# The end of layer 1: other scalar steps, the first twelve row sums of x times M on VectorE, and the squares of M summed by ScalarE

## The chip, the cores and the metric

The kernel runs on one core of one Trainium2 chip. The metric is the device time of one execution, in microseconds (us). The kernel before takes 496.52 us, the median of three runs (496.17 to 497.64).

A core has five engines that work at the same time and wait for each other by semaphores: TensorE (PE in the profile; PEld are its weight loads) multiplies matrices into a memory of eight banks called PSUM, VectorE (DVE), ScalarE (ACT) and GpSimd (POOL) do elementwise work, and SyncE (SP) issues most transfers from main memory.

## The reference

There are 3327 nodes with 64 features (x) and one dense weighted adjacency matrix `adj` (3327 x 3327). Four graph layers follow each other, each as `x = layernorm(x + gnn(x))`. Cut to what matters here:

```python
# layer 0:  x - 0.1 x + const per row
# layer 1, hyperbolic:
x_tan     = logmap0(x)
left      = x_tan @ att_W[:64] + att_b
right     = x_tan @ att_W[64:]
adj_att   = sigmoid(left + right.T) * adj
x_local   = logmap(x[:, None], x[None, :])           # every pair of nodes
support_t = einsum('ij,ijd->id', adj_att, x_local)
out       = proj(expmap(support_t, x))               # contains tanh(|support|)
# layer 2:  twice  x = tanh(concat([adj @ x, x], 1) @ W[k])
# layer 3:  decayed weights of the last 100 neighbours of each row, times (x @ weight), plus bias
```

For every pair of nodes in layer 1 `logmap` gives the direction from i to j in the ball: a number that depends on the pair times x_j, and another one times x_i. After the sum over j each row is therefore a combination of two vectors: of M, the weighted sum of the neighbours' vectors, and of x of the row itself. All that follows the sum (expmap, proj, the residual and the layer norm) needs per row only a few scalars: q, the sum of squares of M's row; p, the sum of x times M over the row; and t, M's last coordinate, which carries the sum of the weights. From these come two factors, alpha and beta, and the layer's output is alpha M + beta x, both centred.

## The kernel before

**Tiling.** The 3327 nodes are padded to 3328, which is 26 blocks of 128. The blocks are kept in pairs, b and b + 13, one in the upper and one in the lower half of the 128 partitions where a tile is transposed: such a tile has 64 + 64 partitions and 13 groups of 128 columns. A "slot" is the place of one block, a "group" is a pair of slots. Scalars per node are tiles of 128 x 26. The transposed tiles are worked on in four chunks of 416 columns (`CW`).

**Order.** Within layer 1 the orders of TensorE, ScalarE, VectorE and GpSimd are written out by hand (`tc.manual_schedule`): an engine runs its instructions in the order of the program text and waits at each for what it needs. Transfers have their own queue on SyncE. A pool of PSUM banks may take over the place of an earlier pool. It then waits for the last users of that place; for pools with `reuse_waits="tile"` this is kept by tile.

**The pairs, `near_sphere`.** Data that lie near a sphere, as these do, take this branch. Column halves `cp` (2), blocks of neighbours `jb` (26) and chunks within the half `ci` (2) make 104 tiles. For each tile:

- TensorE multiplies transposed left rows `riT` with the transposed neighbours `ljT` into `pq` (`products`, L1405). `ljT[1]` holds the same as `ljT[0]` with the partition halves changed.
- ScalarE takes an arctangent of it (`angle`, L1414) and, for each pair of tiles, the sigmoid `sg` of the attention (L1378). GpSimd multiplies `sg` by the adjacency `at` (L1383).
- VectorE makes the weights `v` (`gather`). For even tiles this is one instruction (L1429), for odd ones three (L1425, L1426, L1427).
- TensorE adds v times the block's rows `lj` to `acc` (`collect`, L1449), one PSUM bank for each chunk of the half. When the last block of a half is done, `acc` is copied to `mT`, chunk by chunk (L1455). `mT` is M, transposed. The last two of these copies come after the last tile, the first two in the middle of the layer, where the column half changes.

**The start of the branch.** The transposed operands are made at once, by transpositions into PSUM (`bank`, `alone`, `made`) followed by a copy to `riT`, `ljT[0]`, `ljT[1]` or `lfT`. `right` makes `ljT[0]`, `wrong` makes `ljT[1]` (its first tile is first_wrong in the profile), `turn` makes `riT`, `left_rows` makes `lfT`, which goes through main memory to spread `left` over the partitions. Where `right` copies a part of `ljT[0]`, two transfers on SyncE's queue (`change_over`) make the same part of `ljT[1]`. `seventh` is the last such part of the start: its tile, prep_right, stands in the first `acc` bank, and `by_rows` copies `lfT` from `prep_few`, which stands in the second `acc` bank. Both copies are in VectorE's order behind v of tile 0.

**The tail of the tiles.** Beside the last four tiles GpSimd makes `xm`, which is `mT` times `riT`, for the first half of the columns (L1632) and some scalars per row (`gs`, `gk`, `gsp`, `gs2`, `aav`). TensorE turns the first six groups of `mT` back to rows, by a product with the constant `all_m` (L1645), into `pq_early`: each group gives 128 columns of M and two of t. ScalarE squares these 768 values (`sq_e`, L1650) and copies t (`t_e`, L1654), ahead of the last two copies of `mT`. VectorE makes three scalars per row (`inv_s`, `rxn`, `xn`, L1657 to L1659), the second half of `xm` (L1661), and the row sums of `sq_e` (L1662), which are the first twelve columns of q.

**The end, `near_end`.** It has new pools on the PSUM banks of `acc` and `pq`. In TensorE's order stand: `pm` for groups 6 to 12 (L1720); `pe`, which is p of all 13 groups, each a product of 128 columns of `xm` with a constant of two columns, so 13 products, each shown as two records (L1740); `first_w` (a transposition of `all_m` and the product of the centring matrix with W, L1791 and L1792); `pm` for groups 0 to 2; `second_w` (W times the turned `all_m`, giving `w_m`, and the centred layer 3 weights `w3`, L1802 and L1803); `x_w`, centred x times W of most groups; `pm` for groups 3 to 5; more `x_w` and `m_w`, M times W (`times`, L1760). ScalarE squares `pm` into `sq_m` (L1734), copies M out (`m_out`, L1730) and `x_w` to `lj` (`x_out`, L1766). VectorE sums `sq_m` (L1778, L1779) and runs a chain of short steps of 128 x 26, of which this is the head:

```python
vec(k, p, gs, mul)            # L1786, e_k: the first that needs pe
vec(gp, p, gsp, mul)
vec(k, k, gt, add)
```

From this follow `u2` (the square of the length of support), `ux`, the argument of tanh, tanh on ScalarE (L1824) with two loads of function tables, of which the second is made early by a dummy instruction, e_warm; then `root` and its Sqrt on ScalarE (e_on_s, L1857), a second Sqrt (L1858 has both reciprocals), `alpha` and `beta`. Last comes, per part, `lj = alpha (M W) + beta (x W)` (L1895 to L1897). It is first done for group 0 alone.

**What comes behind.** Layer 2 needs this `lj`: its products with the adjacency (`cnt`, L517) begin with slot 0. The adjacency itself arrives by transfers that run ahead, four blocks of 1664 KB at a time.

## Time and profile before

| | |
|---|---|
| median of the runs | 496.52 us |
| the profiled execution | 496.15 us |
| its span, first to last instruction | 494.3 us |
| granted clock of TensorE, mean | 0.984 |
| TensorE busy | 478.6 us (97%) |
| VectorE busy | 349.8 us (71%) |
| ScalarE busy | 266.1 us (54%) |
| GpSimd busy | 196.8 us (40%) |
| pairs of layer 1 | about 21 to 189 us |
| end of layer 1, `pm` to `cnt` | 189.28 to 203.64 us |
| layers 2 and 3 | 203.64 to 494.3 us |

The span is measured from the first to the last instruction of one execution under the profiler; that execution itself took 496.15 us, so 1.85 us lie around the span. In all the rows that are shown, times are in microseconds, and "L1449" is line 1449 of the kernel before. In a timeline a row has the start, the length, the engine, the line, the operation, the output and input names with shape and type, and the number of instructions in it; in square brackets is the idle time just before and what ended it. A matrix product in float32 appears as two records. In the rows of the chain of waits only what set the end is listed: each row is followed back from the last instruction to what released it, or to what stood before it on its engine.

### The profile page before, as it was taken

How to read it: one execution, taken by the hardware profiler on the slowest of the kernel's cores; microseconds unless marked ns; L12 is line 12 of the kernel's file. 1: busy time of each engine (PE TensorE's matmuls, PEld its weight loads, DVE VectorE, ACT ScalarE, POOL GpSimd, SP SyncE). 2: the span in 40 equal slices, each digit the busy share in tenths (PEclk: the TensorE clock that was granted, in tenths of full speed). 3: DMA queues.
4: the chain of work that ended last, by engine and by line, in shares of the span. 5: the costliest groups of instructions: out<-in, count | busy, mean ns of one | idle time of the engine just before them, and what ended most of it. 6: DMA issues, size and time to landing. Idle time of an engine off the chain costs nothing.

```text
span 494.3 us, 7739 instructions
## 1 busy us (share of the span) xinstructions
PE 478.6 (97%) x2865; PEld 219.2 (44%) x2865; DVE 349.8 (71%) x600; ACT 266.1 (54%) x376; POOL 196.8 (40%) x175
## 2 busy tenths in 40 slices
PE   7999999999999999999999999999999999999991
PEld 4733333334333338644333353333345455555551
DVE  6888888878888887995544322645239999789743
ACT  4899999999999985300000000000016876676641
POOL 4398999989999991000000000000342274000000
PEclk9899999999999998999999999999999999999996
DMA  9998988887888178999998009998997699949001
GB/s 289 358 299 289 321 271 268 267 274 256 280 277 276 71 290 312 427 420 430 420 411 333 0 19 393 428 354 324 422 361 225 227 343 373 384 159 355 16 1 42
DMA packets 34186, 139.20 MB, mean 282 GB/s; under 512 B 11231, under 2 KB 13025, under 8 KB 29019
## 3 DMA queue, kind: packets, MB, share of 16 engines
q1 hardware_dynamic: 30603, 137.41, 74.3%
q10 hardware_dynamic: 2288, 0.57, 0.6%
q0 software_dynamic: 1248, 0.64, 0.6%
q8 instruction: 24, 0.39, 0.3%
q14 instruction: 23, 0.19, 0.1%
HBM read 136.93 MB, written 1.04 MB: 279 GB/s over the span
## 4 chain that ended last, share of the span: by engine, by line
PE 90%; DVE 4%; DMA 1%; issue 1%; ACT 0%; POOL 0%; DVEq 0%
PE cnt L517 30%; PE pq L1405 17%; PE acc L1449 16%; PE cnt L654 6%; PE acc L886 6%; PE acc L903 3%; PE t L452 2%; DVE mask L368 1%; PE both L755 1%; PE cnt L508 1%; DMA mask<-t_rows 1%; PE x_w L1760 1%; DVE w L670 1%; PE pn_l L403 1%; PE pm L1720 1%; PE m_w L1760 1%
## 5 line engine op out<-in xcount | busy, mean ns | idle before, releaser
L1383 POOL TENSOR_TENSOR sg<-sg,at 128x832 f32<-128x832 f32 x88 | 131.5, 1518 | 7.4 <-ACT sg L1378 3.3
L517 PE MATMUL cnt<-at_l,lj 128*64 128x416 f32 x496 | 90.7, 515 | 0.0
L1378 ACT ACTIVATE sg<-lb,rb 128x1664 f32<-128x1664 f32 (+1 forms) x53 | 88.1, 1664 | 0.0
L1405 PE MATMUL pq<-riT,ljT 64*128 64x416 f32 x416 | 87.3, 536 | 0.2
L1449 PE MATMUL acc<-v,lj 128*64 128x416 f32 x416 | 85.1, 525 | 0.0
L1414 ACT ACTIVATE pq<-pq 128x832 f32<-128x832 f32 x104 | 83.9, 852 | 1.7 <-issue 1.6
L633 ACT ACTIVATE x<-cnt 128x416 f32<-128x416 f32 x8 | 4.1, 517 | 143.1 <-PE cnt L517 143.1
L672 ACT ACTIVATE w<-cnt 128x416 int16<-128x416 f32 x135 | 63.9, 519 | 27.3 <-PE cnt L654 25.8
L1429 DVE SCALAR_TENSOR_TENSOR v<-pq,sg 128x832 f32<-128x832 f32 x52 | 53.3, 1025 | 18.7 <-ACT pq L1414 18.4
L464 POOL DMA_DIRECT2D t_rows<-tb x4 | 4.1, 1088 | 150.0 <-DVE tb L462 150.0
L1405 PEld LDWEIGHTS pq<-riT,ljT 64*128 64x128 f32 x416 | 35.6, 186 | 49.5 <-ACT pq L1414 30.6
L517 PEld LDWEIGHTS cnt<-at_l,lj 128*64 128x64 f32 x496 | 34.4, 137 | 49.6 <-issue 49.1
L886 PE MATMUL acc<-w,s 128*128 128x416 bf16 x208 | 53.1, 339 | 0.0
L670 DVE TENSOR_SCALAR w<-cnt 128x416 int16<-128x416 f32 x73 | 42.1, 588 | 11.1 <-PE cnt L654 8.7
L1449 PEld LDWEIGHTS acc<-v,lj 128*64 128x64 f32 x416 | 26.1, 136 | 52.1 <-issue 48.2
L517 PE MATMUL cnt<-kept,lj 128*64 128x416 f32 x224 | 41.4, 515 | 0.0
L368 DVE TENSOR_SCALAR mask<-ah 128x1664 bf16<-128x1664 f32 x34 | 37.2, 1120 | 0.2 <-DMA ah<-in_adjT 0.2
L654 PE MATMUL cnt<-mask,tri 128*128 128x416 bf16 x136 | 35.4, 339 | 1.1 <-DMA mask<-t_rows 0.5
L445 DVE TENSOR_SCALAR tm<-at_l 128x1664 bf16<-128x1664 f32 x16 | 15.7, 1023 | 25.8 <-PE t L452 25.8
L1426 DVE SCALAR_TENSOR_TENSOR pq<-pq,sg 128x416 f32<-128x416 f32 x52 | 31.2, 599 | 1.8
L1425 DVE SCALAR_TENSOR_TENSOR v<-pq,sg 128x416 f32<-128x416 f32 x52 | 30.2, 580 | 0.0
L1047 POOL DMA_DIRECT2D out<-hid x2 | 1.0, 514 | 72.8 <-DVE hid L1052 72.8
(321 smaller groups left out, 522.0 us busy)
## 6 DMA issues: line engine op xcount, KB each, us to landing
at_l<-in_adjT SPq DMA_DIRECT2D x27, 1664.0 KB, 11.7
at<-in_adjT SPq DMA_DIRECT2D x44, 832.0 KB, 6.5
ah<-in_adjT SPq DMA_DIRECT2D x34, 832.0 KB, 6.8
kept<-in_adjT SPq DMA_DIRECT2D x7, 1664.0 KB, 11.0
bt_l<-in_adjT SPq DMA_DIRECT2D x6, 1664.0 KB, 8.7
lb<-lf_rows SPq DMA_DIRECT2D x2, 384.0 KB
mask<-t_rows SPq DMA_DIRECT2D x34, 3.2 KB
ljT<-ljT SPq DMA_DIRECT2D x4, 128.0 KB
```

Source lines behind the costliest of these rows:

```text
L368: nc.vector.tensor_scalar(mask[q], ahead.pop(q), 0.0, None, ALU.not_equal)
L517: nc.tensor.matmul(acc[c][h * D : (h + 1) * D, :], hw[:, slot(jb), :], blocks[jb][:, o : o + CW], start=c not in begun, stop=last, skip_gr ...
L654: nc.tensor.matmul(cnt[c][e], tri, mask[q][:, of], start=True, stop=True, skip_group_check=True,)
L670: nc.vector.tensor_scalar(to, of, 0.0, None, ALU.max)
L672: nc.scalar.activation(to, of, AF.Relu)
L886: nc.tensor.matmul(acc[h, c][:, e, :], s12[:, slot(jb)].rearrange("p t d -> p (t d)"), ws[q, c, e], start=first, stop=last,)
L1378: nc.scalar.activation(sg[:, :, of], lbs[:, :, of], AF.Sigmoid, bias=rb[:, sl : sl + 1])
L1383: nc.gpsimd.tensor_tensor(sg[:, h, of], sg[:, h, of], at[:, h, of], ALU.mult)
L1405: nc.tensor.matmul(pq[:, h, :], ljT[h != jb // NBH][rows, of], riT[rows, ch * CW : (ch + 1) * CW], start=True, stop=True,)
L1414: nc.scalar.activation(pqs[t], pqs[t], AF.Arctan, bias=ANGLE_FIRST, scale=ANGLE_STEP)
L1429: stt(w, pq, ANGLE_REST, sg, op0=ALU.add, op1=ALU.mult)
L1449: nc.tensor.matmul(accs[cp, ci][h * D : (h + 1) * D, :], lj[:, slot(jb), :], w[:, h, :], start=(jb == orders[cp][0]), stop=(jb == orders[c ...
```

## The change

It has four parts. All lie in layer 1.

1. *Start.* `few` moves to the first `acc` bank and `seventh` to the second. The copy of `lfT` comes right behind the first small copies of the start, the copy of prep_right behind v of tile 1, and first_wrong is copied by VectorE.
2. *Change of the column half.* The copy of the second chunk of `mT` goes from ScalarE to VectorE.
3. *Tail of the tiles.* GpSimd makes only the part of `xm` that groups 6 to 12 need, and takes `inv_s`, `rxn`, `xn` and a new scalar `gks`. VectorE multiplies `pq_early` by the centred rows `xc` into `xm_e` and sums it over each row into `p_e`, which gives p of the first twelve slots. ScalarE squares `pq_early` slot by slot, twelve instructions of 128 x 64, each of which also writes the sum of its row to one column of q; four of them come before the copies of `mT` in the text, eight after.
4. *End.* `pe` has seven groups in place of thirteen. The turned `all_m` and `w_m` are gone: `m_w` is M times the same `w_x` that `x_w` uses. w3's scaling is done in its copy from PSUM. `m_out` of groups 0 to 2 stands before tanh, the `x_w` and `m_w` products are in another order, with two copies of `x_w` before Sqrt. The scalar steps are other forms of the same quantities.

```diff
@@ the start
-                    changed()
+                    changed(copy)
...
-                    few = n1c.tile([P, 4 * P], F32, tag="acc1", name="prep_few")
+                    few = n1c.tile([P, 4 * P], F32, tag="acc0", name="prep_few")
...
                     for part in singles:
                         part(copy)
+                    by_rows(copy)
...
-                    seventh = bank(0, right, 5, 4)
+                    seventh = bank(1, right, 5, 4)
...
-                        if t == 0:
-                            seventh(copy)
-                            by_rows(copy)
@@ gather, odd tiles
+                    if t == 1:
+                        seventh(copy)
                     for one in (t - 1, t):
                         collect(one)
@@ collect
-                        sums.append(lambda: nc.scalar.copy(mT[:, of], accs[cp, ci]))
+                        put = nc.scalar.copy if cp or not ci else nc.vector.tensor_copy
+                        sums.append(lambda: put(mT[:, of], accs[cp, ci]))
...
+                def sums_of_squares(pm, first, last):
+                    for sl in range(first, last):
+                        k, h = divmod(sl, 2)
+                        nc.scalar.activation(
+                            sq_e[:, sl], pm[:, k // 3, k % 3, h * D : (h + 1) * D], AF.Square,
+                            accum_out=lpn[:, sl : sl + 1],
+                        )
@@ the tail of the tiles
-                            of = slice(0, 2 * CW)
+                            of = slice(6 * P, 2 * CW)
                             nc.gpsimd.tensor_tensor(xm[:, of], mT[:, of], riT[:, of], ALU.mult)
...
-                            gp.tensor_tensor(gsp, gsp, gs, ALU.mult)
+                            gp.tensor_tensor(inv_s, vq[:, 1], r2[:, 1], ALU.mult)
+                            gp.tensor_tensor(rxn, r2[:, 0], inv_s, ALU.mult)
+                            gp.tensor_scalar(rxn, rxn, 0.25 / 0.9, None, ALU.mult)
+                            gp.tensor_tensor(xn, aa, rxn, ALU.mult)
+                            gp.tensor_tensor(gks, gk, s, ALU.mult)
+                            gp.tensor_scalar(gks, gks, -2.0, None, ALU.mult)
...
                         if t == len(tiles) - 2:
-                            nc.scalar.activation(
-                                sq_e.rearrange("p (a k h) d -> p a k (h d)", a=2, k=3),
-                                pm[..., :P], AF.Square,
-                            )
                             nc.scalar.copy(
                                 t_e.rearrange("p (a k h) -> p a k h", a=2, k=3), pm[..., P:]
                             )
-                    stt(inv_s, vq[:, 1], -0.5 / 0.9, r2[:, 1], op0=ALU.mult, op1=ALU.mult)
-                    stt(rxn, r2[:, 0], -0.5, inv_s, op0=ALU.mult, op1=ALU.mult)
-                    vec(xn, aa, rxn, ALU.mult)
+                            sums_of_squares(pm, 0, 4)
+
+                    def first(v):
+                        return v[:, :12].rearrange("p (a k h) d -> p a k (h d)", a=2, k=3)
+
+                    vec(first(xm_e), pm[..., :P], first(xc), ALU.mult)
                     for of in (slice(c * CW, (c + 1) * CW) for c in (2, 3)):
                         vec(xm[:, of], mT[:, of], riT[:, of], ALU.mult)
-                    nc.vector.tensor_reduce(lpn[:, :12], sq_e, axis=AX.X, op=ALU.add)
+                    sums_of_squares(pm, 4, 12)
+                    nc.vector.tensor_reduce(p_e, xm_e, axis=AX.X, op=ALU.add)
@@ the end
-                p_of(0, NBH)
+                p_of(6, NBH)
...
-                nc.scalar.activation(w3_dg, w3_dg, AF.Copy, scale=float(2**27))
-                vec(k, p, gs, mul)
-                vec(gp, p, gsp, mul)
+                vec(gta, gt, aa, mul)
+                vec(k[:, :12], p_e, gks[:, :12], mul)
+                vec(k[:, 12:], p, gs[:, 12:], mul)
+                vec(gp, k, gsp, mul)
+                vec(h, k, gta, add)
                 vec(k, k, gt, add)
+                gq = of(mul, gs2, q, "gq")
+                u2 = of(mul, k, h, "u2")
+                ka = of(mul, k, aa, "ka")
+                vec(u2, u2, gq, add)
+                ux = of(sub, gp, ka, "ux")
...
-                nc.tensor.transpose(first[:, :P], all_m[:, :P], ident)
-                nc.tensor.matmul(
-                    first[:, P : 2 * P], center, w2_dg[:, 0, :], start=True, stop=True
-                )
+                nc.tensor.matmul(first[:, :P], center, w2_dg[:, 0, :], start=True, stop=True)
+                nc.tensor.matmul(first[:, P : 2 * P], center, w3_dg, start=True, stop=True)
                 m_and_t(0, 3)
-                nc.scalar.copy(all_mT, first[:, :P])
-                nc.scalar.activation(w_x, first[:, P : 2 * P], AF.Copy, scale=rows_63)
-                second = in_bank("second_w")
-                nc.tensor.matmul(second[:, :P], all_mT, w2_dg[:, 0, :], start=True, stop=True)
-                nc.tensor.matmul(second[:, P : 2 * P], center, w3_dg, start=True, stop=True)
+                nc.scalar.activation(w_x, first[:, :P], AF.Copy, scale=rows_63)
+                nc.scalar.activation(w3_dg, first[:, P : 2 * P], AF.Copy, scale=float(2**27))
+                m_out(0, 3)
...
+                x_of(0)
+                x_of(1)
                 m_and_t(3, 3)
+                x_of(3)
+                x_of(2)
...
                 nc.scalar.activation(th, arg, AF.Tanh, scale=-1.0)
-                nc.scalar.copy(w_m, second[:, :P])
                 warm_e = st("warm")
                 nc.scalar.activation(warm_e[:, :1], ones, AF.Sqrt)
-                m_out(0, 3)
-                uy = of(mul, th, ux, "uy")
-                y2 = of(mul, th, th, "y2")
+                x_out(xs[0], *fours[0])
+                x_out(xs[1], *fours[1])
...
+                mw_of(0)
+                mw_of(1)
+                uy = both(ux, 2.0, th, "uy", mul, add)
                 be = of(mul, th, g2, "be")
+                dn = of(mul, th, u2, "dn")
+                vec(uy, uy, th, mul)
+                stt(dn, ux, 2.0, dn, op0=mul, op1=add)
...
                 r0, r = table_root(root, "on")
-                x_out(xs[0], *fours[0])
-                x_out(xs[1], *fours[1])
+                x_out(xs[3], *fours[3])
+                x_out(xs[2], *fours[2])
```

`mw_of(b)` takes a bank and multiplies four groups of `mT` by `w_x`; the last two of these products come behind `m_out` of groups 3 to 5, as in the kernel before.

## The prediction

> **What bounds the kernel now.** I read the page first, for the bound of the whole:
>
> ```profile
> span 494.3 us, 7739 instructions
> ...
> PE 478.6 (97%) x2865; PEld 219.2 (44%) x2865; DVE 349.8 (71%) x600; ACT 266.1 (54%) x376; POOL 196.8 (40%) x175
> ...
> PE 90%; DVE 4%; DMA 1%; issue 1%; ACT 0%; POOL 0%; DVEq 0%
> ```
>
> TensorE is on the chain for 90% of the span: time is won or lost only where TensorE gets less or more to do, or stands. All edits lie in layer 1, so I then read the chain from 184 to 207 us, the end of layer 1 (start, length, what):
>
> ```profile
> 187.73 1.55 PE acc L1449 x8
> 189.28 1.79 PE pm L1720 x14
> 191.07 2.80 PE pe L1740 x26
> ...
> 195.68 3.19 PE x_w L1760 x16
> ...
> 203.64 3.63 PE cnt L517 x19
> ```
>
> No gap: pm follows acc at once, and layer 2's cnt begins at 203.64. The chain omits ScalarE and VectorE, which are close behind. Their timelines (start, length):
>
> ```profile
> 187.77 0.81 ACT L1650 ACTIVATE sq_e<-pq_early 128x768 f32<-128x768 f32 x1 [2.09 <-PE pq_early L1645]
> ...
> 188.65 0.51 ACT L1455 COPY mT<-acc 128x416 f32<-128x416 f32 x1
> 189.35 0.51 ACT L1455 COPY mT<-acc 128x416 f32<-128x416 f32 x1 [0.19 <-PE acc L1449]
> 190.64 1.04 ACT L1734 ACTIVATE sq_m<-pm 128x384 f32<-128x384 f32 x3 [0.78 <-DVE x L1661]
> ```
>
> ```profile
> 193.90 0.19 DVE L1786 TENSOR_TENSOR e_k<-pe,gs 128x26 f32<-128x26 f32 x1 [0.98 <-PE pe L1740]
> ...
> 202.02 0.30 DVE L1895 TENSOR_TENSOR m_w<-m_w,gs 128x128 f32<-128x128 f32 x1
> ...
> 202.54 0.29 DVE L1897 TENSOR_TENSOR lj<-lj,m_w 128x128 f32<-128x128 f32 x1
> ```
>
> VectorE's scalar chain starts with e_k at 193.90, when pe is done, and gives cnt its first lj at 202.83, 0.8 us before TensorE comes for it. That slack is all there is. The granted clock of two stretches (TensorE's busy time, clock, DMA share, GB/s):
>
> ```profile
> 191.10:193.87 2.77, 2.77 (x27) 1.00 0.91 244
> 195.10:198.50 3.40, 3.40 (x19) 0.50 1.02 432
> ```
>
> After the stretch of pe (matrices times two columns, busy but streaming almost nothing) the clock is halved for 3.4 us, and x_w pays: 16 records take 3.19 us, where 8 of m_w take 0.97.
>
> **The change, part by part.** *Before the end of layer 1.* At the start the chain shows a hole in acc, and at the change of column half one before pq:
>
> ```profile
> 26.09 2.38 PE acc L1449 x8
> 28.47 1.60 PE pq L1405 x8
> ```
>
> ```profile
> 110.11 1.04 DVE v L1429
> 111.19 0.97 PE pq L1405 x4
> 112.16 1.70 PE acc L1449 x8
> 113.86 1.60 PE pq L1405 x8
> ```
>
> Eight acc records take 1.55 elsewhere, so 0.83 us is lost at 26.09: acc waits for v of tile 1, whose last multiplication ends at 27.5 on VectorE behind the copies of prep_right (24.88, a step of 0.6) and lfT (0.2). The change puts lfT ahead, into idle time before riT's copy at 23.05, and prep_right behind v of tile 1. v then ends at about 26.7, but acc of tile 1 now stands in the bank that prep_right occupied and must wait for that copy, to 27.35; 0.5 of the hole stays: -0.3 us (between 0 and -0.8). first_wrong's copy moves from ScalarE to VectorE, where 20.2 to 20.9 lies before the first pq at 21.45: nothing on the path; without that room each 0.1 us of lateness would count. SP's change-over transfers fall behind one load; their columns serve from the ninth pair on, at about 50 us. At 106 us one of two mT copies leaves ScalarE (0.51 us and a wait of 0.19). Its sigmoid and angle come 0.6 us earlier; VectorE makes the copy (0.6) between two steps of v, whose last part then ends at 109.5, before acc's last records at 109.85. Pairs of tiles lie 3.145 us apart, so three after pq's start at 103.95 the next is due at 113.39; it comes at 113.86: 0.5 lost, and won back (0 to -0.5). Together **-0.8**.
>
> *The end: what is removed.* 12 of pe's 26 records at 0.108 us (1.29 us), all_m's transposition (0.17) and w_m's product (0.32): 1.8 us of TensorE. It counts only if TensorE isn't made to stand.
>
> *What is added ahead of pm.* sq_e (one instruction of 0.81) becomes twelve squares of 128x64, each with a row sum as accumulator output. Before shows none with that output. The plain one is bounded by sq_m: 488 ns for 384 columns, 283 for 128, so 0.80 ns a column; e_on_s (26 columns, 198.83) is followed at 198.96, so 0.11 us fixed: 0.16 us each if the sum is free. [...] With a second short instruction it is 0.16+0.11; with one of 203 ns, as e_warm, laid open it is 0.36. I take **0.28**, near the middle case, and keep 0.16 and 0.36.
>
> *Who waits.* As the changed program is built, xm_e (VectorE's product of pq_early with xc) waits for the first four squares, the other eight wait for xm_e, and pm's first multiplication waits for xm_e and for the last of the twelve: its pool takes over the place of pq_early's pool. Before, it waited only for the copy of mT, with sq_e in front of that. Behind pm in TensorE's order stand pe, first_w, x_w, m_w and all of layer 2. So:
> - t_e at 187.77, then four squares: done at 187.89 + 4x0.28 + 0.1 = 189.1. The mT copies end at 189.5 and 189.95.
> - xm_e, 768 columns from PSUM (m_w's 128x512 product takes 0.69, 1.04 ns a column more): 0.96, to 190.1.
> - Eight squares: 190.16 + 8x0.28 + 0.1 = 192.5. pm starts at **192.55 instead of 189.28**: TensorE stands 3.3 us.
> - pm 1.79, pe 14x0.108 = 1.51: to 195.86 (193.86 before).
> - VectorE: the last sq_m ends at 194.9 and the two sums of sq_m (steps of 0.46 and 0.62) follow; k is made at about 196.2, +2.3. p_e's reduction replaces that of sq_e (0.94) and ends by 192.3, covered by pm; uncovered it would add its 0.94.
> - Scalar steps: to tanh 17 instead of 15, in an order with fewer direct successors (0.10 instead of 0.22 apart), 2.1 either way. From tanh to root 20 instead of 22, and 2.04 instead of 2.34: -0.3. The root's Sqrt stands behind two copies of x_w on ScalarE: tanh, table load (1.28), warm and two copies are through 2.5 us after tanh begins, root after 2.5: nothing. alpha then comes at +2.0, the first lj at 204.8.
> - TensorE's own work: first_w and pm 1.1, then 52 records of x_w and m_w at 0.121 and pm 0.7: 203.9. So lj decides: cnt at 204.85, **+1.2**.
> - Moved to POOL: inv_s, rxn, xn and gks, six steps of 0.22 to 0.34 more, against the 1.96 of xm's first half, now 64 columns. It ends at about 187.6, long before use. VectorE was idle at 187.7 to 189.2 anyway.
> - ScalarE's m_out of group 0 and w3's scaling now precede tanh; they end by 197.5 and tanh is due at 198.2. Covered by 0.7; behind it the excess would delay tanh.
>
> *The clock.* The row: the window 191.7 to 195.1 streamed about a fifth of the columns that full clock could, and then came 3.4 us at 0.50. [...] But this trace shows TensorE busy in its window and the clock halved. [...] Bounds: 0 (only x_w, as now) and +3 (two windows in a row). I take **+1.1**.
>
> *Sum.* -0.8 + 1.2 + 1.1 = +1.5 on the profiled execution's own 496.15 (span 494.3 and 1.85 around it), which is 0.4 under the median; on the median of 496.52 that is **498.0**.
>
> **The rivals.** A change of under 0.3% (1.5 us) can hardly be told from none here.
> 1. *The forecast*: 498.0, own range 496.9 to 499.3. For it speaks the wait in the program; against it that the price of the accumulator is not in the trace. Chance 0.45.
> 2. *The squares' sums are free* (not slower): at 0.16 each pm starts 1.4 us earlier, at 191.15, the chain's k comes at +0.9 and, with the 0.3 saved, the first lj at 203.4 and cnt at 203.5 as now; with one cold stretch on x_w, as now, the end costs about 0 and the early gain of 0.8 is left: 495.7. It decides from about 0.21 a square downwards. Chance 0.22; 0.4 of it is faster by over 0.3%.
> 3. *The accumulator lays each square open*: at 0.36 or more pm starts 1 us later still, the standing passes a whole window and two cold stretches follow, +1.2 +1.0 +2.5 -0.8 = +3.9: 500.4. For it: twelve instructions in a row on an engine that TensorE waits for. Chance 0.18.
> 4. *The early gains do not hold*: ScalarE's pair of angle and sigmoid takes 3.1 us, nearly TensorE's 3.145, so what is won could be lost to it; the end as in 1: 498.8. Against it: VectorE waits for ScalarE only 0.3 a pair. Chance 0.15.
>
> **How the numbers follow.** Slower by over 0.3%: 0.7 of case 1, all of 3, 0.8 of 4: 0.62. Within 0.3%: the rest of 1 and 4 and 0.6 of 2: 0.29. Faster: 0.09. The range goes from 495.3, somewhat below case 2, to 500.6, just above case 3.
>
> **What would show it.** A gap of TensorE before pm that ends with the last square; squares 0.28 us apart; xm_e between the fourth and the fifth; pm at some 191.7 (192.55 less 0.8); a clock of 0.50 beginning at 192 to 196; pe of 14 records; acc at 26 us in about 2.0 instead of 2.38; even pairs at 107 to 114. Wrong it would be made by squares under 0.21 us apart, by pm that starts before the last square, or by a clock that stays full.

## The result, and the profile after

The changed kernel takes 498.18 us, the median of 21 runs (496.71 to 500.65). The kernel before, in as many runs beside it, takes 496.76 (495.28 to 498.57). The ratio is 1.0029, with a 95% interval from 1.0016 to 1.0043: the change costs 1.4 us, within 0.8 to 2.1. The forecast was 498.0.

The number is right. How it comes about is only in part what the forecast said, as the stages show. First the page, the lines that answer to those of before:

```profile
span 496.2 us, 7732 instructions
...
PE 476.5 (96%) x2850; PEld 216.9 (44%) x2850; DVE 350.5 (71%) x600; ACT 266.4 (54%) x394; POOL 196.4 (40%) x180
```

TensorE has 2.1 us less to do and the span is 1.9 us longer: TensorE stands (has nothing that it can run) for about 4 us more than before. The chain of waits of the changed kernel shows where at the end of layer 1 (start, length, what):

```profile
192.66 0.41 ACT sq_e L1467 x4
193.07 1.07 issue
...
198.85 0.23 ACT e_tanh L1839
199.09 1.28 ACT L1841
200.38 0.20 ACT e_warm L1841
200.59 0.96 ACT lj L1781 x2
201.55 0.14 ACT e_on_s L1878
...
205.16 0.30 DVE lj L1911
205.46 0.04 issue
205.50 1.61 PE cnt L517 x7
```

Before, this stretch was TensorE without a gap. Now ScalarE and VectorE carry it, from the last squares to the first lj, and cnt waits for that lj. TensorE's timeline has the two gaps (in brackets the idle time and what ended it):

```profile
189.19 1.62 PE L1452 MATMUL acc<-v,lj 128*64 128x416 f32 x8
193.12 1.83 PE L1735 MATMUL pm<-all_m,mT 128*128 128x130 f32 x14 [2.32 <-ACT sq_e L1467]
194.79 1.62 PE L1755 MATMUL pe<-but_last,x 128*128 128x2 f32 x14
...
205.50 0.92 PE L517 MATMUL cnt<-at_l,lj 128*64 128x416 f32 x4 [1.22 <-DVE lj L1911]
```

And the timelines of ScalarE and VectorE show what stands in front of pm:

```profile
190.07 0.23 ACT L1467 ACTIVATION_READ_ACCUMULATOR sq_e<-pq_early 128x1 f32 x1
190.16 0.53 ACT L1459 COPY mT<-acc 128x416 f32<-128x416 f32 x1
190.88 0.51 ACT L1459 COPY mT<-acc 128x416 f32<-128x416 f32 x1 [0.19 <-PE acc L1452]
191.32 0.22 ACT L1467 ACTIVATE sq_e<-pq_early 128x64 f32<-128x64 f32 x1
191.44 0.19 ACT L1467 ACTIVATION_READ_ACCUMULATOR sq_e<-pq_early 128x1 f32 x1
191.53 0.22 ACT L1467 ACTIVATE sq_e<-pq_early 128x64 f32<-128x64 f32 x1
```

```profile
190.33 0.96 DVE L1673 TENSOR_TENSOR xm_e<-pq_early,xc 128x768 f32<-128x768 f32 x1 [1.00 <-ACT sq_e L1467]
```

As forecast, each square that writes its row sum is two instructions on ScalarE. Their pitch is 0.20 us (191.32 to 191.53); the forecast took 0.28. xm_e comes behind the fourth square, the last eight come behind the copies of mT, and pm behind the last of them.

The two profiles by stage, from TensorE's and VectorE's rows ("acc done" is the start of the last acc row plus 1.55, the length of such a row in the chain of waits; "the scalar chain" begins with e_k before, at 193.90, and with the new step e_gta after, at 196.70):

| us | before | after | difference |
|---|---|---|---|
| start of the span to the first pq | 21.45 | 23.29 | +1.84 |
| first pq to acc done | 167.76 | 167.45 | -0.31 |
| acc done to pm | 0.00 | 2.38 | +2.38 |
| acc done to the scalar chain | 4.69 | 5.96 | +1.27 |
| acc done to the first lj | 13.62 | 14.71 | +1.09 |
| acc done to cnt (the tail) | 14.36 | 14.76 | +0.40 |
| cnt to the end | 290.8 | 290.7 | -0.1 |

The largest difference, +1.84 at the start, is no effect of the change that these profiles could show. It is the clock:

```profile
14.20:17.60 3.40, 3.13 (x14) 2.27 (x13) 2.78 (x15) 1.38 (x4) 0.00 (x0) 0.50 0.84 219
189.20:192.60 3.40, 3.40 (x32) 3.39 (x31) 3.24 (x9) 1.55 (x4) 0.00 (x0) 1.00 0.48 93
195.10:198.50 3.40, 3.40 (x19) 3.40 (x18) 3.04 (x27) 2.23 (x5) 0.00 (x0) 0.50 1.02 432
```

```profile
15.00:22.00 7.00, 6.21 (x37) 5.14 (x36) 4.52 (x12) 5.59 (x9) 1.95 (x2) 0.51 1.03 379
189.20:192.60 3.40, 1.60 (x9) 0.47 (x8) 2.40 (x5) 3.12 (x24) 0.17 (x1) 1.00 0.34 145
196.00:206.00 10.00, 8.78 (x76) 8.34 (x77) 8.70 (x60) 7.01 (x17) 0.19 (x2) 1.00 1.00 421
```

These are stretches of the kernel before (first fence) and of the changed one (second): length, busy time of TensorE, of its weight loads, of VectorE, ScalarE and GpSimd, then TensorE's granted clock, the DMA share and GB/s. Before has one cold stretch of 3.4 us at the start and one at the end of layer 1. After has two in a row at the start and none at the end. Of the fourteen profiles taken here (these two and those below), five have a single cold stretch there (first pq at 21.45 to 21.89) and nine have two (22.36 to 23.29); both kinds occur with the start as before and with the changed one. The last stage, cnt to the end, also moves, between 290.2 and 291.5 us, though nearly all of it is code that no variant touches. So a difference of two single profiles says little about 1 us here, and every reading below takes the stages apart and adds the runs.

The runs also have a clock, the mean over the execution. Of the changed kernel's 21 runs, 13 have 0.983 to 0.986 and a median of 497.72; 8 have 0.980 or less and a median of 499.57. Below, a run of at most 0.981 is called a low-clock run. Of 148 runs of the kernel before that ran beside the variants below, 25 are such, with a median of 497.7 against 497.0 of the others. This is a rough sign of a cold tail: the mean also takes in the cold stretches at the start and behind the last products, and the kernel before's own profile has a mean of 0.984 with a cold window in its tail. So a run above 0.981 can have one too.

### The profile page after: what moved, and what is told of

The parts are those of the page before. It is cut to its first block, busy times and chain, and to the rows that moved or that the text cites. A ratio compares the mean times of both kernels' runs of the same rounds, so it can differ in the third digit from the quotient of the medians.

```text
span 496.2 us, 7732 instructions
## 1 busy us (share of the span) xinstructions
PE 476.5 (96%) x2850; PEld 216.9 (44%) x2850; DVE 350.5 (71%) x600; ACT 266.4 (54%) x394; POOL 196.4 (40%) x180
## 4 chain that ended last, share of the span: by engine, by line
PE 52%; DVE 5%; ACT 1%; DMA 1%; issue 1%; POOL 0%; ACTq 0%
PE cnt L517 30%; PE cnt L654 6%; PE acc L886 6%; PE acc L903 3%; PE t L452 2%; DVE mask L368 1%; PE both L755 1%; PE cnt L508 1%; DMA mask<-t_rows 1%; DVE w L670 1%; PE pn_l L403 1%; PE pr_o L943 1%; PE cnt L943 0%; DVE sq L803 0%; ACT L1841 0%
```

## The experiments

The theories, by the letters of the expectations. **A**: TensorE's stand before pm sets the loss. In its fuller form, **A2**, it costs twice, by itself and through the clock: a window of 3.4 us in which TensorE works little is followed by a cold one, and where pm, pe and x_w run cold the tail is much longer. **E**: only the wait itself counts. **C**: the stand is not what decides, and cold stretches that have nothing to do with it (such as those of the start) make the loss. **B** and **D**: other parts of the change make it or fail to gain (the early edits; the scalar steps and the order of ScalarE's copies). All ratios are to the kernel before, run beside on the same chip. The rows themselves were not all run side by side: the kernel before has a median of 496.76 beside the changed kernel and of 497.09 to 497.25 beside the variants, so a difference of two medians in this table is uncertain by some 0.5 us.

| kernel | runs | median | ratio (95%) | low-clock runs | pm after acc done | tail in its profile |
|---|---|---|---|---|---|---|
| changed kernel | 21 | 498.18 | 1.0029 (1.0016 to 1.0043) | 8 | 2.38 | 14.76 |
| early_only | 22 | 496.57 | 0.9989 (0.9976 to 1.0002) | 2 | 0.00 | 14.37 |
| end_only | 12 | 499.29 | 1.0030 (1.0006 to 1.0054) | 5 | 2.37 | 18.31 |
| whole_square | 7 | 495.52 | 0.9956 (0.9941 to 0.9971) | 0 | 0.57 | 13.21 |
| plain_squares | 22 | 496.24 | 0.9972 (0.9960 to 0.9983) | 0 | 1.64 | 13.91 |
| double_squares | 6 | 501.81 | 1.0100 (1.0081 to 1.0120) | 6 | 4.01 | 19.62 |
| fill | 13 | 498.39 | 1.0026 (1.0013 to 1.0039) | 0 | 3.86 | 16.21 |
| fill_3 | 22 | 497.06 | 1.0000 (0.9989 to 1.0011) | 0 | 2.46 | 14.82 |
| copied_rows | 14 | 496.79 | 0.9996 (0.9983 to 1.0009) | 8 | 0.00 | 14.77 |
| copied_rows_x | 14 | 496.88 | 1.0002 (0.9988 to 1.0016) | 5 | 0.00 | 15.67 |
| rows_2 | 10 | 495.55 | 0.9969 (0.9955 to 0.9983) | 1 | 0.00 | 12.59 |
| rows_2_fill | 22 | 495.77 | 0.9980 (0.9970 to 0.9990) | 0 | 0.00 | 12.62 |
| x_out_first | 12 | 497.20 | 0.9999 (0.9981 to 1.0016) | 5 | 0.00 | 14.25 |

**early_only.** The kernel before with the edits of the start and of the column half alone (the first part of the diff above, and `put`).

> The kernel before with only the edits at the start of layer 1 and at the change of column half (few and prep_right in other banks, their copies moved, first_wrong and the second chunk of mT copied by VectorE). Theory A (the forecast): these gain 0.8 us, at least 0.4, so 495.9 to 496.4 against 496.76, and acc of tile 1 and the pairs at the change show it. Rival B (the early gains do not hold, because ScalarE's or VectorE's work takes them back): the same as before within 0.3 us.

Measured 0.9989, which holds both -0.8 us and none. Its profile is sharper: from the first pq to acc done it takes 167.47 us instead of 167.76, and every variant with these edits takes 167.44 to 167.47. So the gain is 0.3 us, of which the start has 0.08 and the change of column half 0.23. Why the start gains so little stands in TensorE's and VectorE's rows of the changed kernel:

```profile
27.86 0.92 PE L1452 MATMUL acc<-v,lj 128*64 128x416 f32 x4
29.31 0.92 PE L1452 MATMUL acc<-v,lj 128*64 128x416 f32 x4 [0.53 <-DVE ljT L1532]
```

```profile
28.07 0.59 DVE L1428 TENSOR_TENSOR v<-pq,kept 128x416 f32<-128x416 f32 x1
28.57 0.68 DVE L1532 COPY ljT<-prep_right 128x512 f32<-128x512 f32 x1
```

v of tile 1 is ready at 28.66, 5.37 after the first pq instead of 6.05. But prep_right's copy now stands behind it, and acc of tile 1 waits for that copy, because the bank is its own: it starts 6.02 after the first pq, where it could start at 6.10 before.

This profile shows a second thing. Its tail takes 14.37 us with the end of the kernel before and a clock of 1.00 over x_w (195.60 to 199.00); the kernel before took 14.36 with a clock of 0.50 there. Between these two profiles the cold stretch cost nothing:

```profile
196.13 1.95 PE L1761 MATMUL x_w<-w_x,ljT 128*128 128x128 f32 x16
197.92 0.83 PE L1721 MATMUL pm<-all_m,mT 128*128 128x130 f32 x6
198.59 0.39 PE L1761 MATMUL x_w<-w_x,ljT 128*128 128x128 f32 x2
200.43 1.16 PE L1761 MATMUL m_w<-w_m,mT 128*128 128x128 f32 x8 [1.45 <-ACT lj L1767]
```

The kernel before has, in the same view:

```profile
195.47 3.40 PE L1760 MATMUL x_w<-w_x,ljT 128*128 128x128 f32 x16
```

x_w is 1.45 us quicker with the full clock, and then m_w waits 1.45 for the first copy of x_w, whose bank it takes over and which stands behind root's Sqrt on ScalarE.

**end_only.** The changed kernel with the start and the column half as before.

> The changed kernel with the start and the change of column half as in the kernel before; only the tail and the end are changed. Theory A: the twelve squares hold pm for 2.3 us, the end costs 1.2 us plus what the clock adds, about +1.6 to +2.3 us against before, so 0.4 to 0.8 us slower than the whole change. Rival B (early edits do nothing): the same time as the whole change, +1.4. Rival C (the loss sits at the start, where the profile of the changed kernel shows two cold stretches in a row): +0.3 or less.

Measured 1.0030, too wide to tell the 0.3 us of the early edits. Its profile is one of a low-clock run, and shows what the clock does to this tail:

```profile
190.10:193.50 3.40, 1.09 (x10) 0.98 (x9) 2.53 (x5) 2.18 (x17) 0.00 (x0) 1.00 0.39 82
193.50:196.90 3.40, 3.40 (x19) 3.40 (x17) 1.72 (x7) 1.68 (x4) 0.00 (x0) 0.50 0.91 380
196.90:200.30 3.40, 3.40 (x17) 3.40 (x17) 1.87 (x15) 1.31 (x5) 0.00 (x0) 0.50 1.02 421
200.30:203.70 3.40, 3.40 (x18) 3.40 (x18) 2.18 (x20) 2.55 (x6) 0.00 (x0) 0.50 0.98 419
```

In the first stretch TensorE works 1.09 of 3.40 us, since the stand of 2.3 lies in it whole; the next is cold. And the cold does not end after one window: pe streams two columns for each load of 128, the windows behind the stand hold 1020, 930 and 1450 columns (counted below), and the clock is half from 193.49 to 203.73, three windows long. The tail takes 18.31 us, 3.6 more than with the clock up. In the changed kernel's own profile the windows fall otherwise: acc ends 1.55 us into the one that begins at 189.2, TensorE works 1.60 of it, and the tail stays warm. The same tail, the same stand; where the window falls decides (it is counted below). Rival C, which laid the loss on the start, expected 0.3 us or less of this kernel; it has 1.5 (0.3 to 2.7), which speaks against C but does not yet exclude it.

**whole_square.** One Square of 768 columns in place of twelve.

```diff
-                            sums_of_squares(pm, 0, 4)
+                            nc.scalar.activation(
+                                sq_e.rearrange("p (a k h) d -> p a k (h d)", a=2, k=3),
+                                pm[..., :P], AF.Square,
+                            )
...
-                    sums_of_squares(pm, 4, 12)
+                    nc.vector.tensor_reduce(lpn[:, :12], sq_e, axis=AX.X, op=ALU.add)
                     nc.vector.tensor_reduce(p_e, xm_e, axis=AX.X, op=ALU.add)
```

> The changed kernel with the twelve accumulating squares replaced by the one Square of 128x768 of the kernel before, ahead of the copies of mT, and its row sums on VectorE between xm and p_e's reduction. Theory A: pm no longer waits for squares, only for xm_e and the last mT copy; it starts some 0.8 us after acc instead of 2.3. VectorE has 0.95 more, so the scalar chain starts 0.9 us earlier than in the changed kernel, and layer 2 too: about 0.9 us faster than the changed kernel, +0.5 against before. Rival C (only the clock's cold stretches made the loss): within 0.3 us of the changed kernel. Rival D (the other order of ScalarE's x_w copies and of the scalar steps made it): also within 0.3.

pm starts 0.57 after acc done, released by xm_e:

```profile
189.52 1.80 PE L1738 MATMUL pm<-all_m,mT 128*128 128x130 f32 x14 [0.50 <-DVE xm_e L1676]
```

The chain starts 4.40 after acc done, 1.56 sooner than in the changed kernel; the forecast of 0.9 was too low. The median is 2.7 us below the changed kernel's and the ratio 0.9956: more than the tail's 1.55, and no low-clock run is left. Rivals C and D fall: all the rest of the change, its scalar steps and its orders, is in this kernel, and it is faster than the kernel before. Its stages say what that rest is worth: against the kernel before the chain starts 0.29 sooner after acc done, the first lj is there 0.46 sooner (13.16), and cnt follows that lj at once, where TensorE had 0.74 of its own work left; 1.15 in all.

**plain_squares.** The twelve squares without `accum_out`, and a reduction of `sq_e` on VectorE behind p_e's.

> The changed kernel with the twelve squares as they stand but without their accumulator output; VectorE sums the squares in one reduction behind p_e's. It prices the accumulator. Theory A: a square then takes 0.10 us instead of 0.20 (the profile of the changed kernel shows a second instruction, the accumulator's reading, behind each), the eight squares behind the mT copies are done 0.8 us earlier, pm starts 0.7 to 0.8 us earlier, and the time is 0.7 us below the changed kernel. Rival C: no difference.

Eight squares now take 1.05 us in a row, with a pitch of some 0.12, and pm starts 1.64 after acc done, 0.74 sooner, as expected. The tail is 0.85 shorter, the median 1.9. Again the runs gain about 1 us more than the profile's stages do, and again there is no low-clock run, of 22.

**double_squares.** The last eight squares are made twice (`sums_of_squares(pm, 4, 12)` a second time).

> The changed kernel with the last eight accumulating squares made twice, so that TensorE's stand before pm grows by 8 x 0.20 = 1.6 us to 4.0. Theory A2: where the tail is warm it grows by 1.6; more runs fall cold; against the changed kernel +1.6 to +2.6 us. Rival C (the wait is not what decides): less than +0.5 us.

The stand grows to 4.01, and all six runs are low-clock runs: 501.81, 3.6 above the changed kernel, more than was expected. In its profile TensorE works 0.50 of the 3.40 us ahead of the cold, and the clock is half from 192.41 to 202.65:

```profile
188.90:192.30 3.40, 0.50 (x4) 0.00 (x0) 2.90 (x5) 3.21 (x27) 0.00 (x0) 1.00 0.40 89
```

**fill, fill_3.** Five, and then three (`range(3)`), products whose result nobody uses, on TensorE between the last acc and pm. The wait itself stays.

```diff
+                    idle = n1q.tile([P, 2, 512], F32, tag="pq", name="idle_fill")
+                    for i in range(5):
+                        nc.tensor.matmul(
+                            idle[:, i % 2, :CW], ident, mT[:, :CW], start=True, stop=True,
+                        )
                     sums_of_squares(pm, 4, 12)
```

> The changed kernel with five extra products of 128 columns by 416 on TensorE (their result is not used) between the last acc and pm, where it stands for 2.4 us. pm still waits for the last square. Theory A2 (the stand costs twice: the wait itself, and, in a third to a half of the runs, a window of few columns in front of pm and so a cold clock over pm, pe and x_w, which the profile of the end-only variant shows with a tail of 18.3 us instead of 14.8): the wait stays, the cold runs go, no run has a mean clock of 0.98 or less, and the median falls by 0.5 to 1 us to about 497.4. Rival E (only the wait itself counts): no change against the changed kernel, or slower by what the products run over.

The five were sized wrongly: each takes 0.75 us, they run 1.5 over, and pm starts 3.86 after acc done. The warm tail is 16.21, 1.45 longer than the changed kernel's. And yet the median is only 0.2 higher, and no run has a low clock. Rival E, which expected the whole overrun in the time, does not fit; that the clock gives back what the products cost does.

> The changed kernel with three unused products between the last acc and pm. The five of the earlier variant took 3.76 us, 1.4 more than the stand, so three take 2.26 and stay within it. Theory A2 (the stand brings a cold clock over the tail in part of the runs): tail warm in every run, 14.8 us in the profile, no run with a mean clock of 0.98 or less, and a median 0.9 to 1.3 us below the changed kernel, so about equal to the kernel before. Rival E (only the wait counts): the same as the changed kernel, +1.2 to +1.4 against before.

Three products fit, and this is the cleanest test of A2 against E:

```profile
190.15 2.36 PE L1678 MATMUL idle_fill<-mT,ident 128*128 128x416 f32 x6
192.62 1.80 PE L1740 MATMUL pm<-all_m,mT 128*128 128x130 f32 x14
194.26 1.62 PE L1760 MATMUL pe<-but_last,x 128*128 128x2 f32 x14
...
204.98 1.27 PE L517 MATMUL cnt<-at_l,lj 128*64 128x416 f32 x6 [1.23 <-DVE lj L1916]
```

pm, the chain, lj and cnt come as late as in the changed kernel (tail 14.82 against 14.76), and TensorE only does useless work in place of none. The ratio is 1.0000 (0.9989 to 1.0011), and 0 of 22 runs have a low clock. So of the changed kernel's 1.4 us nothing is left that these runs can measure (they tell 0.5 us) when the clock stays up: its loss is the clock's, and the wait alone, set against the early gain, comes to +0.40 - 0.31 = +0.1. Rival E falls. One thing stays open: the changed kernel's 13 runs with the higher mean clock have a median of 497.72, still 0.7 above fill_3 (of which some 0.5 is the uncertainty of such a difference). Single cold windows among them, which the mean clock does not set apart, would make that; no profile of such a run was taken.

**copied_rows, copied_rows_x.** A form of the change without the wait: ScalarE copies pq_early to SBUF at once, into the place in x2 where these rows must go anyway; the product with xc (GpSimd) and the squares read it there.

```diff
                             nc.scalar.copy(
+                                xm[:, : 6 * P].rearrange("p (a k w) -> p a k w", a=2, k=3),
+                                pm[..., :P],
+                            )
...
-                    vec(first(xm_e), pm[..., :P], first(xc), ALU.mult)
+                    nc.gpsimd.tensor_tensor(
+                        xm_e.rearrange("p n d -> p (n d)"), xm[:, : 6 * P],
+                        xc[:, :12].rearrange("p n d -> p (n d)"), ALU.mult,
+                    )
...
+                first_squares(0, 4)
                 squares(6, 3)
                 squares(9, 3)
                 squares(12, 1)
+                first_squares(4, 12)
...
-                m_and_t(0, 3)
-                m_out(0, 3)
-                m_and_t(3, 3)
-                m_out(3, 3)
```

> The changed kernel in another form: ScalarE copies pq_early once (0.8 us) into x2, from where GpSimd makes the product with xc and ScalarE, four before sq_m and eight behind it, the twelve accumulating squares; the products pm of groups 0 to 5 and their copies on ScalarE (m_out) go, since x2 holds those rows already. Theory A: pm waits for nothing but the mT copies, as in the kernel before; VectorE has one product less than in the variant with one whole square, whose tail took 13.21 us, so the tail takes 12.7 and the whole is 2.0 us below the kernel before or more. Rival F (GpSimd's product or the eight late squares hold the scalar chain): a tail of 13.2 or more.

A miss: 0.9996, a tail of 14.77. pm waits for nothing, but rival F holds, in two places.

```profile
189.93 2.25 DVE L1670 TENSOR_TENSOR x<-mT,riT 128x416 f32<-128x416 f32 x2 [1.36 <-ACT mT L1459]
```

```profile
189.42 1.82 POOL L1665 TENSOR_TENSOR xm_e<-x,xc 128x768 f32<-128x768 f32 x1 [0.83 <-ACT t_e L1661]
```

```profile
193.69 0.39 PE L1816 MATMUL first_w<-both_m 128*128 128x128 f32 x2
196.50 4.80 PE L1769 MATMUL x_w<-w_x,ljT 128*128 128x128 f32 x26 [2.42 <-ACT w_x L1818]
```

VectorE's two products for xm take 2.25 us beside GpSimd's product; in the changed kernel, without it, they take 1.08. They end at 192.18, and GpSimd's ends at 191.24: VectorE seems to have waited for it (an estimate from these times; no row shows the wait). And w_x's copy stands behind the eight late squares and m_out on ScalarE, so TensorE waits 2.42 us for it. That stand is followed by a cold window in turn (a clock of 0.52 from 196.50 to 199.90), and 8 of 14 runs have a low clock.

> The variant with copied rows, and one of the two copies of x_w that stand between tanh and Sqrt on ScalarE moved ahead of tanh. If those copies hold Sqrt (in the profile of the changed kernel Sqrt's input is there at 201.32 and Sqrt begins at 201.55), 0.2 us less than the variant with copied rows; if x_w's products are not done when tanh's argument is, the copy delays tanh, and it is slower by up to 0.5 us.

A ratio of 1.0002 against 0.9996: no difference that these runs can show. Both are held by the same w_x, so the question of Sqrt stays open.

**rows_2, rows_2_fill.** The same, mended: VectorE makes xm_e from SBUF, and `m_out` of groups 6 to 12 moves behind the copies of `w_x` and `w3`. rows_2_fill has one unused product of 384 columns between first_w and x_w.

```diff
-                    nc.gpsimd.tensor_tensor(
+                    vec(
                         xm_e.rearrange("p n d -> p (n d)"), xm[:, : 6 * P],
...
-                m_out(6, 3)
-                m_out(9, 3)
-                m_out(12, 1)
...
                 nc.scalar.activation(w3_dg, first[:, P : 2 * P], AF.Copy, scale=float(2**27))
+                m_out(6, 3)
+                m_out(9, 3)
+                m_out(12, 1)
```

> The variant with copied rows, mended: the product with xc is made by VectorE (GpSimd's had doubled VectorE's time for xm beside it), and w_x is copied ahead of m_out (it had come 2.4 us late for TensorE). pm for groups 0 to 5 stays out. Theory A: the scalar chain starts 3.9 us after acc instead of 4.4 in the variant with one whole square, the tail takes 12.7 us where it is warm. With less for TensorE to stream between pe and x_w, theory A2 expects cold runs: a mean clock of 0.982 or less in a third of the runs or more, and a median 1 to 1.5 us below before.

> As the one before it, with one unused product of 128 columns by 384 on TensorE between first_w and x_w, where it waits for w_x's copy. Theory A2: it keeps the clock up; no runs with a low clock, a tail of 12.7 to 12.9 us, a median 1.8 to 2.2 us below the kernel before, and 0.5 below the variant without the product. Rival E (no effect of the clock): 0 to 0.2 slower than without it.

pm follows acc at once, the chain starts 3.79 after acc done, the tail takes 12.59 and 12.62, as expected: 1.75 less than before. Both are faster than the kernel before, by 0.3% (0.17 to 0.45) and 0.2% (0.1 to 0.3), which is less than the 1.8 to 2.2 us that was expected of rows_2_fill. The low-clock runs that were expected of rows_2 did not come (1 of 10), so the unused product had nothing to win back, and it gains nothing. Why they did not come is not shown: TensorE's wait for w_x is only 0.80 us there, but by the count of columns below a cold window is possible in this kernel too. Of rows_2, rows_2_fill and whole_square the intervals overlap; which is best is not settled.

**x_out_first.** early_only with one more line moved at the end.

```diff
-                r0, r = table_root(root, "on")
                 x_out(xs[0], *fours[0])
+                r0, r = table_root(root, "on")
```

> The kernel before with the early edits, and at the end one line moved: the first copy of x_w on ScalarE goes ahead of the Sqrt that waits for root, where ScalarE stands idle for 0.55 us. In the profile of the early-only variant TensorE waits 1.45 us, with a warm clock, for this copy before m_w can take over its bank. Theory G (this wait, and not x_w's cold clock, sets the end of the kernel before, and the other order of the changed kernel is what takes it away): m_w starts 0.8 us earlier and the first lj at 13.6 us after acc becomes what decides, so the tail falls from 14.37 to 13.7 where it is warm, about 0.6 us less than the early-only variant, 1.0 to 1.3 below the kernel before. Rival H (the end of the kernel before is set by TensorE's own work and clock): the tail stays at 14.4 us and the time at that of the early-only variant, 0.3 to 0.7 below before.

Not settled by the runs: 0.9999 (0.9981 to 1.0016). In the profile m_w follows x_w at once and the wait of 1.45 is gone, as theory G says. But this profile has a cold stretch over x_w (195.84 to 199.26), and the tail takes 14.25, so the 13.7 that G expected of a warm tail was not seen. The runs look alike: 7 with a clock of 0.983 and more have a median of 496.2, the 5 low-clock ones 498.0, a step of 1.8, where the kernel before has 0.7. With the wait gone, a cold clock would no longer be covered by it; this would explain the larger step, but twelve runs are few for it.

## Why the prediction was right, and by which steps

The total was right, its largest terms were not. The sum was -0.8 (early) +1.2 (end) +1.1 (clock) = +1.5. The profiles give -0.3 and +0.4, and the ratios of the changed kernel and fill_3 differ by 1.4, the clock's part; that makes +1.5 too. The early gain was taken 0.5 too large, the cost of the end 0.8 too large and that of the clock 0.3 too small. These errors cancel, and that the number came out this close is in good part luck. Of the forecast's own three signs of being wrong, two came true in the profile: the squares are under 0.21 apart, and at the end of layer 1 the clock stays full. What holds is the mechanism: TensorE stands before pm until the last square (2.38), cnt comes later by it (0.40), and the clock makes it dearer (1.4).

- **The hole at the start, -0.3.** Measured -0.08. The forecast saw that acc of tile 1 would wait for prep_right's copy. By its own times (27.5 without the change, 27.35 with it) this left 0.15 to gain, not 0.3: the subtraction was made against the length of the hole, not against the end of the wait.
- **The column half, -0.5.** Measured -0.23. The last part of v, behind VectorE's copy, ends as forecast: at 111.27 in the changed kernel, whose first pq is 1.84 later and which has won 0.08, so at 109.5 on the time scale of before. But the forecast held this against acc's last records at 109.85. The odd tile's four records, the second half of acc, need it, and they were due from about 109.4: acc of that pair takes 1.86 us instead of 1.62, and half of what is won is lost there.
- **The square, 0.28.** Measured 0.20 with the second instruction, 0.12 without. There is a second instruction, as was suspected, but the time is nearer to the free case (0.16) than to the value taken. Twelve times 0.08 is 1.0, and the stand is 2.4 instead of 3.3.
- **lj decides, +2.0 for lj and +1.2 for cnt.** lj came 1.09 later, by the shorter stand, and so cnt 0.40. The mechanism (cnt waits for lj; TensorE has spare time) is as forecast: TensorE waits 1.22 before cnt. The scalar steps between tanh's argument and lj were taken as 0.3 shorter and are 0.2 shorter.
- **m_out and w3 ahead of tanh, covered by 0.7.** They were done 0.70 us before tanh. **Sqrt behind two copies, nothing.** Its input is written at 201.32 (the row of e_root: 201.13 and 0.19), and the reciprocal that needs its result begins 0.39 later, at 201.71; before, 0.29 lie between the two (198.80 and 199.09). So it costs 0.1, inside lj's +1.09, and is why the 0.3 that the steps save (2.28 instead of 2.59 from tanh to root) arrives as 0.2.
- **The clock, +1.1.** No run shows this term: it is the author's choice between 0 and +3, and the runs give 1.4 in its place. Nor does each run have a cold stretch in the tail: the changed kernel's own profile has none, and 8 of its 21 runs have a low mean clock. Where it came in a profile with this tail (end_only) it was three windows and 3.6 us, more than was taken; the mean over the runs is of the forecast's size. Where the windows fall decides: in the changed kernel's profile the first one has part of acc in it, the two hold 1740 and 1840 columns (counted below), and the clock stayed up. So there is not one time: the runs lie about 497.7 and 499.6, and the median is mostly of the first.
- **Where a cold stretch falls.** In end_only it falls on pm in part (2.52 us, in the changed kernel 1.83), on pe (2.98, there 1.62) and on 16 records of x_w (3.62, there 2.00). In the kernel before it falls on x_w, and between early_only's profile and that of before it cost nothing (a tail of 14.37 and of 14.36), since m_w waited for x_w's copy anyway. The forecast read x_w's 3.19 us as a price that was paid.
- **Rivals.** The second (free sums) was to decide from 0.21 a square downwards; the square took 0.20, so its condition held, and still the kernel is slower: it had counted with one cold stretch that costs nothing. Its start for pm is also too early: at 0.16 a square the last eight stand behind the mT copies at 189.95 and end at 191.33, not 191.15. The third (two cold stretches) did not have its condition, squares of 0.36, but its end came where the stand was made longer: double_squares has three cold windows in its profile and a low clock in every run, 501.81. The fourth did not occur: what was won early was kept until the end of the pairs.

Which windows are followed by a cold one, the fourteen profiles allow to count. In each of them the edges of all cold stretches lie whole multiples of 3.413 us apart (in the kernel before 17.59, 195.09, 198.50 and 485.22: 52, 1 and 84 of them), so that the windows run on by themselves there. For each window the columns of the matrix products in it are added up: 416 for a record of 128x416, times the share of a 128x128 block of weights that it uses (a half for 128x64), and in part where a record lies partly inside.

| kernel | window | TensorE busy, us | columns | clock of the next window |
|---|---|---|---|---|
| before | 191.67 to 195.09 | 3.41 | 1380 | half |
| before | 195.09 to 198.50 | 3.41 | 2090 | full |
| early_only | 190.26 to 193.67 | 3.41 | 1780 | full |
| changed kernel | 189.12 to 192.54 | 1.69 | 1740 | full |
| changed kernel | 192.54 to 195.95 | 2.83 | 1840 | full |
| end_only | 190.08 to 193.49 | 1.10 | 1020 | half |
| end_only | 193.49 to 196.90 | 3.41 | 930 | half |
| end_only | 196.90 to 200.32 | 3.41 | 1450 | half |
| end_only | 200.32 to 203.73 | 3.41 | 2060 | full |
| double_squares | 188.99 to 192.41 | 0.41 | 370 | half |

It comes out without exception behind the first 5 us of the execution (ahead of that, windows with fewer columns stayed warm): of 1991 windows the 67 with 1515 columns or less are followed by a cold one, the 1924 with 1567 or more by a warm one, whatever their own clock. So here busy time does not tell: the columns do (with TensorE busy for 3.41 us and 930 columns the next window is cold in end_only, with 1.69 us and 1740 it is warm in the changed kernel). All windows near the limit hold float32 products, in which a window of cnt reaches about 4090 columns, so the limit is some three eighths of that; how products of other types count is not shown. The forecast's "about a fifth" for the window from 191.7 us is 1380 of the 8085 columns that the fullest window of that profile holds (at 444 us, products of bf16): 0.17.

Where the windows would fall can be tried on the rows of a profile, by moving the 3.413 us grid over them (an estimate, for the rows as they are). In whole_square, plain_squares, fill, fill_3 and rows_2_fill no position gives the tail a window under 1705 columns, and these five have no low-clock run, of 86. In double_squares every position gives one under 1515. In the changed kernel about half of the positions do, or a quarter if acc's half-width products are counted in full, which separates the windows as well; in the kernel before, where it is covered, some two thirds; in rows_2 over four tenths.

## What to carry to other kernels

A stand of TensorE in front of thin work (loads with few columns behind each) can cost more than its length: 1.63 us more of it cost 3.6 in double_squares. Count how many columns the 3.4 us around it stream, wherever the window may fall, and where some positions fall short (here of 1515 to 1567) expect two times for one program rather than one (497.72 and 499.57 in the changed kernel). Before an engine's instruction is split to give it a second output, look which pool takes over the tile that it reads: one early copy out of PSUM (rows_2) or one whole Square ahead of the copies (whole_square) freed the bank here, and made the rest of the change a gain (ratios of 0.9969 and 0.9956). With the first pq at 21.45 to 23.29 us in the fourteen profiles, by one or two cold windows at the start, one pair of profiles misleads about the total; take the stages that the clock leaves alone (first pq to acc done repeats within 0.03 us among the kernels with the early edits), and runs for the rest.

## What the hardware showed that was not expected

- A cold stretch renews itself: at half the clock a window of pe, first_w and pm holds only 930 to 1450 columns (end_only), too few to end it, and three in a row occur (193.49 to 203.73 in end_only, 192.41 to 202.65 in double_squares).
- Useless work can pay: with three products of 2.3 us in all (fill_3) the median is 1.1 us lower (1.4 by the ratios), and no low-clock run is left.
- A Square of 128x64 with a row sum has a second instruction on ScalarE and a pitch of 0.20 us from PSUM, 0.24 from SBUF (copied_rows); without the sum it is some 0.12 (plain_squares).
- VectorE's two products of SBUF operands took twice as long beside GpSimd's product of 128x768 (copied_rows) as without it (the changed kernel), 2.25 against 1.08. VectorE's end lies 0.94 behind GpSimd's, a little less than the 1.08 that its products take alone.
- A product of 128x128 by 416 columns in float32 takes 0.75 us (fill: 3.76 for five), twice the 0.39 of acc's with 64 columns of weights (1.55 for four products in eight records).
